# Gated cross-attention: x loaded a second time and transposed in 32x32 blocks on VectorE, scores computed transposed on two column halves of TensorE, tokens in pairs of tiles

## The chip, the cores and the metric

The kernel runs on one core of a Trainium2 chip. The metric is the device time of one execution in microseconds; lower is better. The time of the kernel before is the median of three runs, and one more execution was taken with the hardware profiler. All arithmetic is in 32-bit floats, in both kernels.

## What is computed

There are 8 batches of 1024 tokens with 1024 features (`x`), and for each batch 64 rows of memory with 512 features (`ctx_1024`).

```python
memory_proj = einsum('bme,de->bmd', memory, W_mem)                 # [8, 64, 1024]
scores = einsum('bnd,bmd->bnm', x, memory_proj) / sqrt(1024)       # [8, 1024, 64]
attn = softmax(scores, axis=-1)
memory_context = einsum('bnm,bmd->bnd', attn, memory_proj)         # [8, 1024, 1024]
gate_input = concatenate([x, memory_context], axis=-1)
gate = sigmoid(einsum('bnf,df->bnd', gate_input, W_gate) + b_gate) # W_gate [1024, 2048]
fused = x + gate * memory_context
out = fused * rsqrt(mean(fused**2, axis=-1) + 1e-6) * norm_w
```

## The kernel before

With mp = memory @ W_mem.T and W_gate = [W1 | W2], the second half of the gate's product is attn @ (mp @ W2.T). So a first stage computes, once for all batches, `mpT` (mp transposed, features on partitions: lines 108 to 122) and `mg` (for each batch 64 rows of mp over 64 rows of mp @ W2.T + bias: lines 124 to 153). This stage is the same work in both kernels; the steps that matter in it are the transposition of the memory into `memT` (`pt_mem`, L103 and L106), the product `pm` (L112) and the products `pg` of L142, whose results VectorE adds to the bias (L151).

Then come the tokens: 64 tiles of 128 tokens, four tiles to a group of 512, 16 groups. For each group `g`:

- `xg` holds its 512 rows of x, tokens on partitions, loaded in one transfer of 2 MB (`load_x`, four buffers).
- `scores(g, t)`: TensorE needs x with features on partitions. Eight transpositions of 128x128 (`pt`, L169) turn one tile; VectorE (L171) and ScalarE (L173) copy each half from PSUM into `xt` (two buffers, one for each of two groups). Then eight products of `xt` with `mpT` (L175) give the scores `sc` of the tile, 128 tokens on partitions by 64 columns.
- `softmax(g)`: over the group's four tiles at once, on VectorE and ScalarE; it writes `attn`.
- `transpose_attn(g)`: four transpositions on TensorE (`pa`, L206), and a copy on VectorE to `attnT` (L208).
- `fuse(g, t)`: 16 products of `xt` with W1 (`pg`, L223: eight for each of two halves of 512 columns), and then four products with 64 rows: two give the context `pc` (L235, rows 0 to 63 of the array), two add the gate's second half to `pg` (L236, rows 64 to 127). Sigmoid on ScalarE (L241), two multiplications and an addition on VectorE (L242, L243), the sum of squares on ScalarE (L244).
- `norm(g)`: square root on ScalarE, then one scaling for each tile on VectorE (L253) and its store.

The loop over the groups does `scores` and `softmax` of group g+1 between the tiles of `fuse` of group g. The order on each engine is made by a scheduler from the program, and each engine then runs its own queue in that order; SyncE (SP) issues all DMAs in order. In the trace every f32 product is two instructions on TensorE, each with its own weight load (a row with x16 is eight products); a transposition is one.

Of the kernel before, what the change touches and what calls it, by code (L numbers as in the profile page):

```python
# [8 lines left out]
F32 = mybir.dt.float32  # L9
# [5 lines left out]
P = 128  # L15
# [4 lines left out]
def tile_gated_cross_attention_rmsnorm(  # L20
    ctx: ExitStack,
    tc: tile.TileContext,
    x: bass.AP,  # [B, N, D]
    mem: bass.AP,  # [B, M, E]
    w_mem_t: bass.AP,  # [E, D]   W_mem transposed
    w_gate_t: bass.AP,  # [2D, D]  W_gate transposed
    b_gate: bass.AP,  # [D]
    norm_w: bass.AP,  # [D]
    out: bass.AP,  # [B, N, D]
):  # L30
    """Tokens lie on partitions, in groups of GT = 512.
# [10 lines left out]
    GT = 512  # L42
    TPG = GT // P  # tiles of 128 tokens in a group
    GPB = N // GT  # groups in a batch
    NG = B * GPB
# [5 lines left out]
    SCALE = 1.0 / float(D) ** 0.5  # L51

    const = ctx.enter_context(tc.tile_pool(name="const", bufs=1))
    xpool = ctx.enter_context(tc.tile_pool(name="xpool", bufs=4))
# [3 lines left out]
    ps_tr = ctx.enter_context(tc.tile_pool(name="ps_tr", bufs=2, space=PSUM))  # L58
    ps_sc = ctx.enter_context(tc.tile_pool(name="ps_sc", bufs=1, space=PSUM))
# [4 lines left out]
    mem_sb = xtpool.tile([P, NPAIR, E], F32, tag="xt", name="mem_sb")  # L64
    nc.sync.dma_start(mem_sb, mem.rearrange("b m e -> (b m) e").rearrange("(q p) e -> p q e", p=P))
    wm_sb = xpool.tile([P, KE, D], F32, tag="xg", name="wm_sb")
    nc.sync.dma_start(wm_sb, w_mem_t.rearrange("(k p) d -> p k d", p=P))

    def load_x(g):
        b, n0 = g // GPB, (g % GPB) * GT  # L70
        xg = xpool.tile([P, TPG, D], F32, tag="xg", name=f"xg{g}")
        nc.sync.dma_start(xg, x[b, n0 : n0 + GT, :].rearrange("(t p) d -> p t d", p=P))
        return xg

    xgs = {0: load_x(0)}

    bias_sb = const.tile([P, D], F32, name="bias_sb")
    nc.sync.dma_start(bias_sb, b_gate.partition_broadcast(P))
    w2_sb = []
    for h in range(NH):  # L80
        t = xpool.tile([P, KD, H], F32, tag="xg", name=f"w2_{h}")
        nc.sync.dma_start(t, w_gate_t[D:, h * H : (h + 1) * H].rearrange("(k p) f -> p k f", p=P))
        w2_sb.append(t)
    w1_sb = const.tile([P, KD, D], F32, name="w1_sb")
    for k in range(0, KD, 2):
        nc.sync.dma_start(
            w1_sb[:, k : k + 2, :],
            w_gate_t[k * P : (k + 2) * P, :].rearrange("(k p) f -> p k f", p=P),
        )
# [9 lines left out]
    memT = xtpool.tile([P, KE, BM], F32, tag="xt", name="memT")  # L99
    for k in range(KE):  # L100
        pt = ps_tr.tile([P, BM], F32, tag="tr", name=f"pt_mem{k}")
        for q in range(NPAIR):
            nc.tensor.transpose(  # L103
                pt[:, q * P : (q + 1) * P], mem_sb[:, q, k * P : (k + 1) * P], ident
            )
        nc.vector.tensor_copy(memT[:, k, :], pt)  # L106

    mpT = const.tile([P, KD, BM], F32, name="mpT")
    for d in range(KD):
        pm = ps_gate.tile([P, BM], F32, tag="gate", name=f"pm{d}")  # L110
        for k in range(KE):
            nc.tensor.matmul(  # L112
                pm,
                wm_sb[:, k, d * P : (d + 1) * P],
                memT[:, k, :],
                start=(k == 0),
                stop=(k == KE - 1),
            )
        if d % 2 == 0:
            nc.scalar.copy(mpT[:, d, :], pm)  # L120
        else:
            nc.vector.tensor_copy(mpT[:, d, :], pm)

    mg = const.tile([P, B, D], F32, name="mg")
    for q in range(NPAIR):
        for h in range(NH):
            cols = slice(h * H, (h + 1) * H)
            pt = ps_tr.tile([P, H], F32, tag="tr", name=f"pt_mp{q}_{h}")
            for j in range(H // P):
                nc.tensor.transpose(  # L130
                    pt[:, j * P : (j + 1) * P],
                    mpT[:, h * (H // P) + j, q * P : (q + 1) * P],
                    ident,
                )
            for i in range(2):
                nc.scalar.copy(mg[0:M, 2 * q + i, cols], pt[i * M : (i + 1) * M, :])  # L136
# [19 lines left out]
    xts, scs, attns, attnTs = {}, {}, {}, {}  # L156

    def scores(g, t):
        """x transposed, and the scores [128 tokens, M] of one tile."""
        b = g // GPB  # L160
        if t == 0:
            xts[g] = xtpool.tile([P, KD, GT], F32, tag="xt", name=f"xt{g}")
            scs[g] = ps_sc.tile([P, TPG, M], F32, tag="sc", name=f"sc{g}")
        xg, xt, sc = xgs[g], xts[g], scs[g]
        toks = slice(t * P, (t + 1) * P)
        for c in range(0, KD, 4):
            pt = ps_tr.tile([P, 4, P], F32, tag="tr", name=f"pt{g}_{t}_{c}")
            for j in range(4):
                nc.tensor.transpose(pt[:, j, :], xg[:, t, (c + j) * P : (c + j + 1) * P], ident)  # L169
            if c == 0:  # L170
                nc.vector.tensor_copy(xt[:, c : c + 4, toks], pt)  # L171
            else:
                nc.scalar.copy(xt[:, c : c + 4, toks], pt)  # L173
        for k in range(KD):
            nc.tensor.matmul(  # L175
                sc[:, t, :],
                xt[:, k, toks],
                mpT[:, k, b * M : (b + 1) * M],
                start=(k == 0),
                stop=(k == KD - 1),  # L180
            )

    def softmax(g):
        """attn of a group, twice side by side so that its transpose fills both row groups."""
        sc = scs.pop(g)
        mx = small.tile([P, TPG], F32, tag="mx", name=f"mx{g}")
        nc.vector.tensor_reduce(mx, sc, AX.X, ALU.max)
        e = small.tile([P, TPG, M], F32, tag="e", name=f"e{g}")
        nc.vector.tensor_tensor(e, sc, mx.unsqueeze(2).to_broadcast([P, TPG, M]), ALU.subtract)
        nc.scalar.activation(e, e, AF.Exp, scale=SCALE)  # L190
        den = small.tile([P, TPG], F32, tag="den", name=f"den{g}")
        nc.vector.tensor_reduce(den, e, AX.X, ALU.add)
        rden = small.tile([P, TPG], F32, tag="rden", name=f"rden{g}")
        nc.vector.reciprocal(rden, den)
        attn = small.tile([P, TPG, 2, M], F32, tag="attn", name=f"attn{g}")
        for i in range(2):
            nc.vector.tensor_tensor(
                attn[:, :, i, :], e, rden.unsqueeze(2).to_broadcast([P, TPG, M]), ALU.mult
            )
        attns[g] = attn  # L200

    def transpose_attn(g):
        attn = attns.pop(g)
        pa = ps_sc.tile([P, TPG, P], F32, tag="sc", name=f"pa{g}")
        for t in range(TPG):
            nc.tensor.transpose(pa[:, t, :], attn[:, t, :, :].rearrange("p i m -> p (i m)"), ident)  # L206
        attnT = small.tile([P, TPG, P], F32, tag="attnT", name=f"attnT{g}")
        nc.vector.tensor_copy(attnT, pa)  # L208
        attnTs[g] = attnT

    sss = {}

    def fuse(g, t):
        """xg[:, t] becomes x + gate * context, and its sum of squares is taken."""
        b = g // GPB
        if t == 0:
            sss[g] = small.tile([P, TPG], F32, tag="ss", name=f"ss{g}")
        xg, xt, attnT, ss = xgs[g], xts[g], attnTs[g], sss[g]
        pgs = []
        for h in range(NH):  # L220
            pg = ps_gate.tile([P, H], F32, tag="gate", name=f"pg{g}_{t}_{h}")
# [10 lines left out]
        for h in range(NH):  # L232
            cols = slice(h * H, (h + 1) * H)
            pc = ps_ctx.tile([P, H], F32, tag="ctx", name=f"pc{g}_{t}_{h}")
# [3 lines left out]
        gate = work.tile([P, D], F32, tag="gate", name=f"gate{g}_{t}")  # L238
# [7 lines left out]
    def norm(g):  # L246
        b, n0 = g // GPB, (g % GPB) * GT
        xg, ss = xgs.pop(g), sss.pop(g)
        rstd = small.tile([P, TPG], F32, tag="rstd", name=f"rstd{g}")
        nc.scalar.activation(rstd, ss, AF.Sqrt, bias=eps_sb, scale=1.0 / D)  # L250
        nc.vector.reciprocal(rstd, rstd)
        for t in range(TPG):
# [4 lines left out]
        del xts[g], attnTs[g]  # L257

    for t in range(TPG):
        scores(0, t)  # L260
    softmax(0)
    transpose_attn(0)
    for g in range(1, min(3, NG)):
        xgs[g] = load_x(g)
    for g in range(NG):
        nxt = g + 1 < NG
        for t in range(TPG):
            if nxt:
                scores(g + 1, t)
                if t == TPG - 1:  # L270
                    softmax(g + 1)
            fuse(g, t)
        if nxt:
            transpose_attn(g + 1)
        norm(g)
        if g + 3 < NG:
            xgs[g + 3] = load_x(g + 3)
# [26 lines left out]
```

## Time and profile before

| | |
|---|---|
| median of three runs | 1310.34 us (1309.6 to 1310.35) |
| the profiled execution: span from the first to the last instruction | 1308.3 us |
| the same execution's own time around the span | not listed; the median of the runs is 2.0 us above the span |
| TensorE products busy (PE) | 1284.8 us, 98% of the span |
| TensorE weight loads busy (PEld) | 644.2 us, 49% |
| VectorE busy (DVE) | 343.4 us, 26% |
| ScalarE busy (ACT) | 288.2 us, 22% |
| DMA | 80.33 MB, 61 GB/s over the span |
| granted TensorE clock | 0.995 (mean) |

How to read the rows. A row of the timeline has the start, the duration (of several merged instructions: from the first start to the last end), engine, line, operation, tiles (out<-in), shape and count; the bracket at the end is the engine's idle time before it and what ended it. A row of the groups has the busy time, the mean duration of one instruction in ns, and the idle time before. A row of the chain has start, duration and what ran. Matmuls are pipelined: the duration of one (594 ns for 512 columns) is longer than the distance between two, so the cost of a run of matmuls is read from the start of the run to the start of what follows it.

### The profile page before, as it was taken

To read this page: it belongs to the slowest core of one execution; us is meant where nothing else is said; L and a number is where in the kernel's file an instruction comes from. 1 tells how busy PE (TensorE), PEld (TensorE's weight loads), DVE (VectorE), ACT (ScalarE), POOL (GpSimd) and SP (SyncE) were. 2 spreads that over 40 slices of the span, in tenths; PEclk is the share of its full clock that TensorE was granted. 3 is DMA by queue.
4 is the path that set the end of the run, shared out by engine and by line. 5 is a ranking of instruction groups with operands and counts; after the bars stand their busy time and mean duration, and the time that the engine had idled before them with its cause. 6 is when DMAs were issued, how large, how long until landed. Compare 5 with 4: busy or idle time off the path is not lost.

```text
span 1308.3 us, 10030 instructions
## 1 busy us (share of the span) xinstructions
PE 1284.8 (98%) x4400; PEld 644.2 (49%) x4400; DVE 343.4 (26%) x472; ACT 288.2 (22%) x435; POOL 0.7 (0%) x7
## 2 busy tenths in 40 slices
PE   7999999999999999999999999999999999999995
PEld 3446555455545544555455545554555445544442
DVE  1122132132314122232313213231312313231413
ACT  0301131122213122122213122221213112221311
POOL 0000000000000000000000000000000000000000
PEclk9999999999999999999999999999999999999998
DMA  9311003030301103030200203030110301010101
GB/s 366 147 65 65 1 1 129 1 129 1 128 1 65 65 1 129 1 129 1 106 23 22 107 1 129 1 129 0 67 62 1 129 1 65 1 65 1 44 21 64
DMA packets 22220, 80.33 MB, mean 61 GB/s; under 512 B 1441, under 2 KB 1441, under 8 KB 22177
## 3 DMA queue, kind: packets, MB, share of 16 engines
q1 hardware_dynamic: 22176, 79.70, 15.8%
q8 instruction: 34, 0.56, 0.2%
q14 instruction: 10, 0.07, 0.0%
HBM read 46.14 MB, written 33.55 MB: 61 GB/s over the span
## 4 chain that ended last, share of the span: by engine, by line
PE 97%; DMA 1%; DVE 1%; ACT 1%; DVEq 0%; issue 0%; SPq 0%; ACTq 0%
PE pg L223 67%; PE pc L235 9%; PE sc L175 9%; PE pt L169 5%; PE pg L142 4%; PE pm L112 2%; DMA wm_sb<-in_w_mem_t 1%; PE pa L206 1%; DVE xg L253 0%; ACT mg L136 0%; PE pt_mp L130 0%; PE pg L236 0%; ACT L250 0%; DVE xg L243 0%; DVEq L300 0%; ACT gate L244 0%
## 5 line engine op out<-in xcount | busy, mean ns | idle before, releaser
L223 PE MATMUL pg<-w_sb,xt 128*128 128x512 f32 x2048 | 903.4, 594 | 0.0
L223 PEld LDWEIGHTS pg<-w_sb,xt 128*128 128x128 f32 x2048 | 379.3, 190 | 431.3 <-issue 429.0
L242 DVE TENSOR_TENSOR gate<-gate,pc 128x512 f32<-128x512 f32 x128 | 86.3, 684 | 791.0 <-ACT gate L241 790.8
L241 ACT ACTIVATE gate<-pg 128x512 f32<-128x512 f32 x128 | 74.8, 597 | 607.6 <-PE pg L236 607.5
L175 PEld LDWEIGHTS sc<-mpT,xt 128*128 128x128 f32 x1024 | 123.0, 192 | 34.2 <-DVE xt L171 24.6
L236 PE MATMUL pg<-mg,attnT 64*128 64x512 f32 x256 | 126.8, 615 | 0.0
L235 PE MATMUL pc<-mg,attnT 64*128 64x512 f32 x256 | 126.8, 615 | 0.0
L175 PE MATMUL sc<-mpT,xt 128*128 128x64 f32 x1024 | 123.0, 273 | 0.0
L244 ACT ACTIVATE gate<-xg 128x1024 f32<-128x1024 f32 x64 | 67.6, 1057 | 109.3 <-DVE xg L243 109.3
L235 PEld LDWEIGHTS pc<-mg,attnT 64*128 64x128 f32 x256 | 42.8, 186 | 78.7 <-issue 78.7
L243 DVE TENSOR_TENSOR xg<-xg,gate 128x1024 f32<-128x1024 f32 x64 | 78.1, 1220 | 1.2
L241 ACT ACT_TABLE_LOAD x31 | 39.8, 1283 | 174.5 <-PE pg L236 174.2
L253 DVE SCALAR_TENSOR_TENSOR xg<-xg,rstd,nw_sb 128x1024 f32<-128x1024 f32 x64 | 77.9, 1279 | 0.6
L169 PEld LDWEIGHTS pt<-ident,xg 128*128 128x128 f32 x512 | 55.9, 142 | 35.5 <-PE pg L236 33.4
L169 PE MATMUL pt<-ident,xg 128*128 128x128 f32 x512 | 69.4, 278 | 0.7 <-ACT xt L173 0.7
L142 PE MATMUL pg<-w,mpT 128*128 128x512 f32 x128 | 55.9, 592 | 0.0
L173 ACT COPY xt<-pt 128x512 f32<-128x512 f32 x64 | 37.6, 587 | 79.8 <-PE pt L169 79.8
L171 DVE COPY xt<-pt 128x512 f32<-128x512 f32 x64 | 44.0, 688 | 9.6 <-PE pt L169 6.7
L236 PEld LDWEIGHTS pg<-mg,attnT 64*128 64x128 f32 x256 | 42.8, 186 | 0.0
L142 PEld LDWEIGHTS pg<-w,mpT 128*128 128x128 f32 x128 | 23.9, 190 | 27.7 <-issue 27.7
L112 PE MATMUL pm<-memT,wm_sb 128*128 128x512 f32 x64 | 29.9, 630 | 1.2 <-DMA wm_sb<-in_w_mem_t 1.2
L151 DVE TENSOR_TENSOR mg<-pg,bias_sb 64x512 f32<-64x512 f32 x16 | 11.0, 690 | 48.9 <-PE pg L142 48.8
(31 smaller groups left out, 177.2 us busy)
## 6 DMA issues: line engine op xcount, KB each, us to landing
xg<-in_x SPq DMA_DIRECT2D x16, 2048.0 KB, 7.8
out<-xg SPq DMA_DIRECT2D x64, 512.0 KB, 2.8
w<-in_w_gate_t SPq DMA_DIRECT2D x2, 2048.0 KB, 22.2
w_sb<-in_w_gate_t SPq DMA_DIRECT2D x4, 1024.0 KB, 16.4
wm_sb<-in_w_mem_t SPq DMA_DIRECT2D x1, 2048.0 KB, 10.2
mem_sb<-in_mem SPq DMA_DIRECT2D x1, 1024.0 KB, 5.6
bias_sb<-in_b_gate SPq DMA_DIRECT2D x1, 512.0 KB, 15.5
nw_sb<-in_norm_w SPq DMA_DIRECT2D x1, 512.0 KB, 16.0
```

Source lines behind the costliest of these rows:

```text
L112: nc.tensor.matmul(pm, wm_sb[:, k, d * P : (d + 1) * P], memT[:, k, :], start=(k == 0), stop=(k == KE - 1),)
L142: nc.tensor.matmul(pg, mpT[:, k, q * P : (q + 1) * P], w2_sb[h][:, k, :], start=(k == 0), stop=(k == KD - 1),)
L169: nc.tensor.transpose(pt[:, j, :], xg[:, t, (c + j) * P : (c + j + 1) * P], ident)
L175: nc.tensor.matmul(sc[:, t, :], xt[:, k, toks], mpT[:, k, b * M : (b + 1) * M], start=(k == 0), stop=(k == KD - 1),)
L223: nc.tensor.matmul(pg, xt[:, k, t * P : (t + 1) * P], w1_sb[:, k, h * H : (h + 1) * H], start=(k == 0), stop=False,)
L235: nc.tensor.matmul(pc, attnT[0:M, t, :], mg[0:M, b, cols], start=True, stop=True)
L236: nc.tensor.matmul(pgs[h], attnT[M:P, t, :], mg[M:P, b, cols], start=False, stop=True)
L241: nc.scalar.activation(gate[:, cols], pgs[h], AF.Sigmoid)
L242: nc.vector.tensor_tensor(gate[:, cols], gate[:, cols], pcs[h], ALU.mult)
L243: nc.vector.tensor_tensor(xg[:, t, :], xg[:, t, :], gate, ALU.add)
L244: nc.scalar.activation(gate, xg[:, t, :], AF.Square, accum_out=ss[:, t : t + 1])
L253: nc.vector.scalar_tensor_tensor(xg[:, t, :], xg[:, t, :], rstd[:, t : t + 1], nw_sb, ALU.mult, ALU.mult)
```

## The change

Five things are changed together.

1. **x comes twice.** Beside `xg` (now 256 rows, a pair of tiles, 1 MB, four buffers) there is `xq` (two buffers): the same 256 rows, laid out so that partition 32i + c holds features 256i to 256i+255 of the tokens whose number is c modulo 32. It is loaded by four DMAs of 32 partitions each, in pieces of 1 KB.
2. **The transposition of x moves to VectorE.** For each pair, eight instructions of 128x256 transpose all 32x32 blocks of `xq` into `xt` (L203). The feature order in `xt` is a permuted one, so W1 and W2 are loaded with their rows in that order (eight DMAs of 32 partitions for each instead of four and two), and the columns of W_mem are permuted by four copies on VectorE (`wmp`, L142). The transpositions L169 on TensorE and the copies L171 and L173 are gone.
3. **The scores are computed transposed.** `mpT` is the stationary side (64 columns) and `xt` the moving one (128 tokens), so that the result is 64x128; the two tiles of a pair go to partitions 0 to 63 and 64 to 127 of one PSUM tile `psT`, on columns 0 to 63 and 64 to 127 of the array (L214). ScalarE copies it to `sT` (L222), and one transposition on TensorE turns it into `sc` (L228), tokens on partitions again.
4. **Pairs instead of groups.** Softmax, `transpose_attn`, `norm` and the stores are done for each of 32 pairs. The copy to `attnT` goes from VectorE to ScalarE (L251).
5. **The order.** `transpose_x` and `scores` of pair q+1 stand ahead of `fuse(q, 0)`, `softmax(q+1)` between the two tiles, `transpose_attn(q+1)` behind the second.

```diff
+    PT = 2 * P
+    PPB = N // PT
+    NQ = B * PPB
-    xpool = ctx.enter_context(tc.tile_pool(name="xpool", bufs=4))
+    big = ctx.enter_context(tc.tile_pool(name="big", bufs=2))
+    xqpool = ctx.enter_context(tc.tile_pool(name="xqpool", bufs=2))
+    xgpool = ctx.enter_context(tc.tile_pool(name="xgpool", bufs=4))
     xtpool = ctx.enter_context(tc.tile_pool(name="xtpool", bufs=2))
-    ps_tr = ctx.enter_context(tc.tile_pool(name="ps_tr", bufs=2, space=PSUM))
-    ps_sc = ctx.enter_context(tc.tile_pool(name="ps_sc", bufs=1, space=PSUM))
+    ps_sc = ctx.enter_context(tc.tile_pool(name="ps_sc", bufs=3, space=PSUM))
...
+    def load_xq(q):
+        b, n0 = q // PPB, (q % PPB) * PT
+        xq = xqpool.tile([P, S, Q4], F32, tag="xq", name=f"xq{q}")
+        src = x[b, n0 : n0 + PT, :].rearrange("(s c) (i e) -> i c s e", c=32, i=4)
+        for i in range(4):
+            nc.sync.dma_start(xq[32 * i : 32 * (i + 1), :, :], src[i])
+        return xq
...
+    wmp = []
+    for k in range(2):
+        t = xqpool.tile([P, 2, KD, P], F32, tag="xq", name=f"wmp{k}")
+        for c in range(2):
+            nc.vector.tensor_copy(
+                t[:, c, :, :].rearrange("p j (i r) -> p j i r", r=32),
+                wm[k][:, c, :].rearrange("p (i j r) -> p j i r", i=4, r=32),
+            )
+        wmp.append(t)
...
-        for c in range(0, KD, 4):
-            pt = ps_tr.tile([P, 4, P], F32, tag="tr", name=f"pt{g}_{t}_{c}")
-            for j in range(4):
-                nc.tensor.transpose(pt[:, j, :], xg[:, t, (c + j) * P : (c + j + 1) * P], ident)
-            if c == 0:
-                nc.vector.tensor_copy(xt[:, c : c + 4, toks], pt)
-            else:
-                nc.scalar.copy(xt[:, c : c + 4, toks], pt)
-        for k in range(KD):
-            nc.tensor.matmul(sc[:, t, :], xt[:, k, toks], mpT[:, k, b * M : (b + 1) * M], ...)
+    def transpose_x(q):
+        xq = xqs.pop(q)
+        xt = xtpool.tile([P, KD, PT], F32, tag="xt", name=f"xt{q}")
+        for s in range(S):
+            nc.vector.transpose(
+                xt[:, :, 32 * s : 32 * (s + 1)], xq[:, s, :].rearrange("p (j r) -> p j r", r=32)
+            )
+        xts[q] = xt
+
+    def scores(q):
+        b, xt = q // PPB, xts[q]
+        ps = ps_sc.tile([P, P], F32, tag="sc", name=f"psT{q}")
         for k in range(KD):
+            for t in range(2):
+                nc.tensor.matmul(
+                    ps[t * M : (t + 1) * M, :],
+                    mpT[:, k, b * M : (b + 1) * M],
+                    xt[:, k, t * P : (t + 1) * P],
+                    start=(k == 0),
+                    stop=(k == KD - 1),
+                )
+        sT = small.tile([P, P], F32, tag="sT", name=f"sT{q}")
+        nc.scalar.copy(sT, ps)
+        sTs[q] = sT
+
+    def softmax(q):
+        sc = ps_sc.tile([P, 2, M], F32, tag="sc", name=f"sc{q}")
+        nc.tensor.transpose(sc.rearrange("p t m -> p (t m)"), sTs.pop(q), ident)
...
-        nc.vector.tensor_copy(attnT, pa)
+        nc.scalar.copy(attnT, pa)
...
+    for q in range(NQ):
+        nxt = q + 1 < NQ
+        if q + 2 < NQ:
+            xqs[q + 2] = load_xq(q + 2)
+            xgs[q + 2] = load_xg(q + 2)
+        if nxt:
+            transpose_x(q + 1)
+            scores(q + 1)
+        fuse(q, 0)
+        if nxt:
+            softmax(q + 1)
+        fuse(q, 1)
+        if nxt:
+            transpose_attn(q + 1)
+        norm(q)
```

How the order moves, at three places (a row has the line, the operation, the tile it writes and those it reads, the shape and how many stand in a row; a number at the end of a name tells one buffer from another).

TensorE in the kernel before, from the last tile of one group to the first of the next; the next group's x is transposed and scored between the gate's products:

```order
L223 MATMUL pg_3_1_629<-w_sb,xt_327 128x512 x8
L235 MATMUL pc_3_0_638<-mg,attnT_426 128x512
L236 MATMUL pg_3_0_620<-mg,attnT_426 128x512
L235 MATMUL pc_3_1_641<-mg,attnT_426 128x512
L236 MATMUL pg_3_1_629<-mg,attnT_426 128x512
L206 MATMUL pa_651<-ident,attn_617 128x128 x4
L169 MATMUL pt_0_0_673<-ident,xg_430 128x128 x4
L169 MATMUL pt_0_4_679<-ident,xg_430 128x128 x4
L223 MATMUL pg_0_0_694<-w_sb,xt_432 128x512 x4
L175 MATMUL sc_672<-mpT,xt_671 128x64 x8
L223 MATMUL pg_0_0_694<-w_sb,xt_432 128x512 x4
```

TensorE in the changed kernel at the end of a pair; `psT_671` are the scores of the pair after the one whose gate products follow (`xt_538`), and its `xt_662` lies in the buffer that the first row reads as `xt_414`:

```order
L266 MATMUL pg_1_1_621<-w_sb,xt_414 128x512 x8
L278 MATMUL pc_1_0_630<-mg,attnT_522 128x512
L279 MATMUL pg_1_0_612<-mg,attnT_522 128x512
L278 MATMUL pc_1_1_633<-mg,attnT_522 128x512
L279 MATMUL pg_1_1_621<-mg,attnT_522 128x512
L249 MATMUL pa_643<-ident,attn_609 128x128 x2
L214 MATMUL psT_671<-xt_662,mpT 64x128 x16
L266 MATMUL pg_0_0_691<-w_sb,xt_538 128x512 x8
```

The score products now stand in one piece at the pair's end, between `pa` and the next gate products, with nothing else for TensorE to do ahead of them.

VectorE in the changed kernel at the same place of a later pair (with what each row waits for: `PE_49` is TensorE, `DMAHW` a transfer). The rows in front are the softmax of the pair before, those behind the elementwise part of the tile whose gate products have just ended:

```order
L240 TENSOR_TENSOR attn_981<-e_974,rden_979 128x2x64
L203 STREAM_TRANSPOSE xt_1034<-xq_903 128x8x32 [waits DMAHW4_49,DMAHW1_49,DMAHW7_49,DMAHW0_49,PE_49]
L203 STREAM_TRANSPOSE xt_1034<-xq_903 128x8x32 x7
L285 TENSOR_TENSOR gate_1_1008<-gate_1_1008,pc_1_0_1002 128x512 [waits Activation_49]
L285 TENSOR_TENSOR gate_1_1008<-gate_1_1008,pc_1_1_1005 128x512 [waits Activation_49]
L286 TENSOR_TENSOR xg_660<-xg_660,gate_1_1008 128x1024 [waits DVE_49]
```

In the kernel before, one PSUM copy of a tile (L171) stood at this place, behind the elementwise rows; now eight transpositions stand ahead of them, and their wait on TensorE is for the last gate product that reads the buffer they write.

VectorE in the changed kernel ahead of the first pair; the rows L190 are the last additions of the first stage (L151 before):

```order
L190 TENSOR_TENSOR mg<-pg_1_3_335,bias_sb 64x512 [waits PE_49]
L190 TENSOR_TENSOR mg<-pg_1_3_335,bias_sb 64x512
L203 STREAM_TRANSPOSE xt_356<-xq_346 128x8x32 [waits DMAHW6_49,DMAHW7_49,DMAHW5_49,DMAHW0_49]
L203 STREAM_TRANSPOSE xt_356<-xq_346 128x8x32 x7
L230 TENSOR_REDUCE mx_386<-sc_384 128x2 [waits PE_49]
```

The first pair's transposition stands behind the last addition, which waits for TensorE's last product of the first stage; in the kernel before, TensorE itself transposed the first tiles there.

More of the change, by code (lines that the diff above doesn't have):

```diff
@@ L196, in softmax, with transpose_attn @@
         for i in range(2):
             nc.vector.tensor_tensor(
-                attn[:, :, i, :], e, rden.unsqueeze(2).to_broadcast([P, TPG, M]), ALU.mult
+                attn[:, :, i, :], e, rden.unsqueeze(2).to_broadcast([P, 2, M]), ALU.mult
             )
[L200 to L205, printed above, removed]
+        attns[q] = attn
+    def transpose_attn(q):
+        attn = attns.pop(q)
+        pa = ps_sc.tile([P, 2, P], F32, tag="sc", name=f"pa{q}")
+        for t in range(2):
@@ L244, in fuse, with norm @@
         nc.scalar.activation(gate, xg[:, t, :], AF.Square, accum_out=ss[:, t : t + 1])
[L246 to L249, printed above, removed]
+    def norm(q):
+        b, n0 = q // PPB, (q % PPB) * PT
+        xg, ss = xgs.pop(q), sss.pop(q)
+        rstd = small.tile([P, 2], F32, tag="rstd", name=f"rstd{q}")
         nc.scalar.activation(rstd, ss, AF.Sqrt, bias=eps_sb, scale=1.0 / D)
         nc.vector.reciprocal(rstd, rstd)
-        for t in range(TPG):
+        for t in range(2):
             nc.vector.scalar_tensor_tensor(
```

151 lines of the change are left out of this document (66 added, 85 removed).

## The prediction

> **What bounds the kernel now.** I read the page's head and its chain first, to see which engine sets the time.
>
> ```profile
> span 1308.3 us, 10030 instructions
> PE 1284.8 (98%) x4400; PEld 644.2 (49%) x4400; DVE 343.4 (26%) x472; ACT 288.2 (22%) x435; POOL 0.7 (0%) x7
> PE 97%; DMA 1%; DVE 1%; ACT 1%; DVEq 0%; issue 0%; SPq 0%; ACTq 0%
> ```
>
> TensorE is on the chain for 97% of the span; what leaves its queue shortens the time, unless a wait takes its place. Busy time misleads for pipelined products, so I price them by distances between starts. Next the chain in order of time over one group (start, duration, what ran):
>
> ```profile
> 191.92 1.93 PE sc L175 x16
> ...
> 206.13 1.02 PE pt L169 x8
> ...
> 208.87 1.73 PE sc L175 x16
> 210.60 12.07 PE pg L223 x28
> ...
> 261.52 0.59 PE pa L206 x4
> ...
> 266.42 1.93 PE sc L175 x16
> ```
>
> The row at 191.92 comes back at 266.42: a group takes 74.50 us, without a gap. Sixteen score instructions take 208.87 to 210.60, or 0.108 each; 28 gate instructions 12.07, or 0.43 each. Last the timeline of TensorE in the last group, where no next group is transposed or scored:
>
> ```profile
> 1229.94 0.66 PE L206 MATMUL pa<-ident,attn 128*128 128x128 f32 x4
> 1230.43 1.02 PE L223 MATMUL pg<-w_sb,xt 128*128 128x512 f32 x2
> ...
> 1246.18 14.00 PE L223 MATMUL pg<-w_sb,xt 128*128 128x512 f32 x32
> 1260.11 0.69 PE L235 MATMUL pc<-mg,attnT 64*128 64x512 f32 x1
> 1260.11 0.69 PE L236 MATMUL pg<-mg,attnT 64*128 64x512 f32 x1
> ...
> 1262.03 1.55 PE L223 MATMUL pg<-w_sb,xt 128*128 128x512 f32 x3
> ```
>
> A tile with its gate and context alone takes 1246.18 to 1262.03, or 15.85 us; both kernels have 64 of these. `pc` and `pg` with 64 rows start together at 1260.11, so two halves of the array run side by side here. Four `pa` transpositions take 0.49 (1229.94 to 1230.43): 0.43 and some 0.06 of changeover.
>
> **The sum, part by part.**
>
> *Removed on TensorE.* A group of 74.50 less four tiles of 15.85 leaves 11.10 for its transpositions, scores and `pa`: 177.6 us for 16 groups. All of it is on the chain.
>
> *Added on TensorE, per pair.* `pa` of two: 0.27. `sc` of one: 0.17. `psT`: 16 products are 32 instructions. Each streams 128 columns where a gate instruction streams 512, so a quarter of 0.43: 0.108. If the column halves run side by side as the row halves do, that is 16 times 0.108 = 1.72; one behind the other it is 3.44. I take 1.72 by the nearest row, the pair at 1260.11, and both as ends. Beyond 3.44 lies an upper end: no overlap at all, each at the duration of a short product alone, 273 ns:
>
> ```profile
> L175 PE MATMUL sc<-mpT,xt 128*128 128x64 f32 x1024 | 123.0, 273 | 0.0
> ```
>
> That is 8.7 us a pair, 225 us more in all. For entering and leaving the halves I add 0.25: a tile has 32 times 0.43 and four times 0.43, or 15.48, and the other 0.37 of the 15.85 is its changeover into row halves and out; here the way in falls into the wait below. The Trainium skill, TensorEngine Tiling (Array Packing), section Key Properties, says that changing the tiling mode drains the engine: the trace agrees by that 0.37, and paying it in full here would add 4 us. The Trainium skill, TensorE: Matmul & The Clock Gate, section "Measured speedup vs the span model", has three 32-column tiles 2.38 times as fast, not three; two halves at the same share of ideal would give 1.6 times, and the sum would be 14 us higher. No row here shows column halves. Together 2.41 a pair, 77.1 for 32 pairs.
>
> *The new wait.* The transpositions of a pair write the `xt` buffer that the gate products just ended have read, and `psT`, next but for the context products and `pa`, needs all eight of them from its second product on. Ahead of it TensorE has only 1.92 (1260.11 to 1262.03) and 0.27. The price on VectorE is not in the trace. Nearest are ops of the same 128x256, and one of twice the length:
>
> ```profile
> L197 DVE TENSOR_TENSOR attn<-e,rden 128x256 f32<-128x256 f32 x32 | 12.2, 422 | 0.6
> L208 DVE COPY attnT<-pa 128x512 f32<-128x512 f32 x16 | 11.0, 684 | 0.8 <-PE pa L206 0.8
> ```
> ```profile
> 622.33 0.76 DVE L197 TENSOR_TENSOR attn<-e,rden 128x256 f32<-128x256 f32 x2
> ```
>
> From 256 to 512 elements an op grows by 262 ns, so about 1.02 ns an element; 1024 would take about 1.2 us. Two independent ops of 256 end in 0.76, 0.34 behind each other. Eight are 7 x 0.34 + 0.42 = 2.8 at that pace, 8 x 0.42 = 3.4 with no overlap; I take 3.1. The bounds lie further out: two elements a step would halve it to 1.6, and four steps an element (a 1024-wide op each) would make it 9.8. The Trainium skill, VectorE: DVE Perf Modes, section The three transpose paths, gives 311 ns for 128x128 in bf16; an estimate of 0.44 for twice the elements would put the sum 13 us higher.
>
> The ends of the wait:
>
> ```profile
> 99.68 1.02 PE L142 MATMUL pg<-w,mpT 128*128 128x512 f32 x2
> 100.74 0.69 DVE L151 TENSOR_TENSOR mg<-pg,bias_sb 64x512 f32<-64x512 f32 x1 [5.47 <-PE pg L142]
> ...
> 616.18 0.69 DVE L171 COPY xt<-pt 128x512 f32<-128x512 f32 x1
> 616.31 0.30 PEld L223 LDWEIGHTS pg<-w_sb,xt 128*128 128x128 f32 x2
> 616.42 1.02 PE L223 MATMUL pg<-w_sb,xt 128*128 128x512 f32 x2
> 616.93 0.19 PEld L175 LDWEIGHTS sc<-mpT,xt 128*128 128x128 f32 x1 [0.32 <-DVE xt L171]
> ```
>
> VectorE starts 0.04 after a product's end, a weight load 0.06 after VectorE's, a product 0.11 after its load. The last gate product of a tile ends at 1260.18 (1246.18 + 14.00); VectorE has nothing else, since the softmax ahead of it ended long before. 1260.18 + 0.04 + 3.1 + 0.17 = 1263.49, against 1260.11 + 1.92 + 0.27 = 1262.30. So TensorE waits 1.2 us, in 30 pairs (the first two have free buffers): 36 us. VectorE's elementwise ops stand behind the transpositions, 3 us later; the PSUM that they free is wanted a tile, 15 us, later.
>
> *Start.* One transfer of W_mem becomes two, and four 1024-wide copies on VectorE must run ahead of most of `pm`.
>
> ```profile
> 6.50 3.84 PE L103 MATMUL pt_mem<-ident,mem_sb 128*128 128x128 f32 x16 [6.50 <-DMA mem_sb<-in_mem]
> 7.62 0.69 DVE L106 COPY memT<-pt_mem 128x512 f32<-128x512 f32 x1 [7.62 <-PE pt_mem L103]
> 11.51 29.91 PE L112 MATMUL pm<-memT,wm_sb 128*128 128x512 f32 x64 [1.17 <-DMA wm_sb<-in_w_mem_t]
> ```
>
> The 2 MB land at 11.5, 5 us after the memory's 1 MB, so the first half at about 9. Then VectorE does four copies of 1.2 and four of 0.69, 7.6 us, to 16.5. By then TensorE has done three products, 2.6 us. It is 16.5 - 2.6 - 11.5 = 2.4 later. At two elements a step it would be about nothing.
>
> *First pair.* At 100.70 TensorE went from L142 straight to `pt`. Now it waits for VectorE's two last additions (0.04 + 2 x 0.69), eight transpositions and 0.17: 4.7 us. The wait of 0.9 that the first group's softmax cost (16 x 74.50 from 100.70 is 1292.7, the products end at 1293.6) goes, since four gate products stand beside that chain now.
>
> *End.* The last `norm` scales two tiles, not four:
>
> ```profile
> 1293.20 0.59 PE L236 MATMUL pg<-mg,attnT 64*128 64x512 f32 x1
> ...
> 1299.45 4.87 DVE L253 SCALAR_TENSOR_TENSOR xg<-xg,rstd,nw_sb 128x1024 f32<-128x1024 f32 x4
> ```
>
> Two of 1.2 are 2.4 less.
>
> *At nothing.* ScalarE's table loads go from 63 to 127, and at
>
> ```profile
> L241 ACT ACT_TABLE_LOAD x31 | 39.8, 1283 | 174.5 <-PE pg L236 174.2
> ```
>
> 64 more are 82 us on an engine that is 22% busy. At a pair's end the sigmoids may come 1.3 later; the gate product that wants their PSUM stands behind `pa`, `psT` and eight gate products (6.9 us). Without that cover it would be 1.3 x 32 = 41 us. The `sT` copy is wanted 15 us later, `attnT` 14. x comes twice, 1 MB more a pair in pieces of 1 KB:
>
> ```profile
> xg<-in_x SPq DMA_DIRECT2D x16, 2048.0 KB, 7.8
> w<-in_w_gate_t SPq DMA_DIRECT2D x2, 2048.0 KB, 22.2
> ```
> ```profile
> 11.50:50.00 38.50, 38.05 (x107) 18.13 (x108) 2.77 (x4) 10.12 (x18) 0.00 (x0) 1.00 0.90 345
> ```
>
> An `xq` buffer is free once its pair is transposed and wanted two pairs later, 70 us. Each pair's last quarter and its `xg` stand in SP's queue behind two stores that wait for `norm`, some 12 us after the pair's end; even 22 us to land leaves 35. W2 is wanted from about 44 us and W1 from 103; at the 345 GB/s of the last row (the stretch 11.5 to 50 us) their 8 MB take 24 us, and they stand ahead of `xq` in the queue. If an `xq` came 10 us late each time it would cost 300 us; I see nothing that makes it so.
>
> *The sum:* 1308.3 - 177.6 + 77.1 + 36 + 2.4 + 4.7 - 0.9 - 2.4 = 1247.6 of span. The median of the runs stands 2.0 above the profiled span: 1250.
>
> **Rivals.** (a) *The column halves run one behind the other.* All eight k-steps read the same 128 partitions for both halves, unlike the row halves at 1260.11, which read different ones. Then 1.72 x 32 = 55 more: 1305. (b) *The transpositions are dear, and it ends slower.* A 32x32 block must be full before it can be written, and 4-byte data may need two passes. At the 684 of a 512-wide op, eight take 5.5, the wait grows by 2.4 in 30 pairs and the first: 1324. It decides from 0.63 us for each: 60 us more over 31 places is 1.94, or 5.04 for eight. Against it: the 128x256 ops all take 422. (c) *The wait is hidden.* With eight transpositions in 1.9 us or less TensorE never waits: 1213. It needs more than one element a step, which no VectorE row here shows. (d) *Both (a) and (b)*: about 1380, or halves that don't overlap at all, to 1475.
>
> **How the numbers follow.** My forecast, side by side and about one element a step, gets 0.60; its own range is 1232 (transpositions at 2.8, W_mem copies twice as fast) to 1276 (the halves 1.6 times as fast, transpositions at 3.6). (a) 0.16, around 1305; (b) 0.13; (c) 0.05; (d) 0.06. The range 1228 to 1318 takes the forecast, nearly all of (a) and the near part of (b). What 0.2% can tell is 2.6 us: faster means below 1307.7. Faster: 0.60 + 0.05 + two thirds of (a) = 0.76; the same 0.05 from (a) and (b); slower 0.19.
>
> **What would show it.** In the changed kernel's groups, L203 at 0.35 to 0.45 us; `psT` in the timeline, pairs of starts 0.108 apart for 1.7 us, and a weight load of L214 that waits for VectorE about 1.2 us at every pair's end, with gate products right behind. The period of a pair should be 35.3 us against 37.25. It would be wrong if L214 takes 3.4 us or more, if L203 takes 0.63 us or more, or if L203 waits for a transfer instead of TensorE.

## The result, and the profile after

The changed kernel takes 1225.81 us (median of 4 runs, 1225.63 to 1226.71), the kernel before 1309.97 in the same comparison: 0.9361 times, with a 95% interval of 0.9348 to 0.9374. The forecast was 1250, in the right direction, 24 us too high, and the result lies 2 us below the low end of its range. The profiled execution has a span of 1223.9 us, 84.4 below the 1308.3 of before.

The head of the page, DMA queue 1, and the chain by engine:

```profile
span 1223.9 us, 9771 instructions
PE 1195.8 (98%) x3920; PEld 541.1 (44%) x3920; DVE 385.8 (32%) x764; ACT 361.1 (30%) x531; POOL 0.7 (0%) x7
q1 hardware_dynamic: 57424, 113.26, 31.3%
PE 91%; DVE 7%; ACT 1%; DMA 1%; issue 0%; DVEq 0%; SPq 0%; ACTq 0%
```

TensorE is busy for 98% of the span, as before, but only 91% of the chain is its own: VectorE, which had 1%, has 7%. The chain in order of time over one pair (start, duration, what ran), and its last product:

```profile
592.37 1.96 PE psT L214 x30
594.33 13.93 PE pg L266 x32
...
610.18 0.26 PE sc L228
610.44 13.75 PE pg L266 x32
624.19 0.02 issue
624.21 2.74 DVE xt L203 x8
626.96 0.04 issue
627.00 1.96 PE psT L214 x30
...
1211.98 0.03 PE pg L279
```

From 592.37 to 627.00 a pair takes 34.63 us; two tiles took 37.25 before, and the forecast was 35.3. At each pair's end the chain leaves TensorE for the eight transpositions on VectorE: 2.74 us, which stand where context products and `pa` run beside them. How much of that is a real wait the timeline of the same place tells (the bracket is the engine's idle time):

```profile
624.21 2.73 DVE L203 STREAM_TRANSPOSE xt<-xq 128x256 f32<-128x256 f32 x8 [9.99 <-PE pg L266]
...
626.02 0.44 PE L249 MATMUL pa<-ident,attn 128*128 128x128 f32 x2
626.39 0.43 PE L214 MATMUL psT<-xt,mpT 128*64 128x128 f32 x2
627.00 1.72 PEld L214 LDWEIGHTS psT<-xt,mpT 128*64 128x64 f32 x30 [0.42 <-DVE xt L203]
627.00 1.96 PE L214 MATMUL psT<-xt,mpT 128*64 128x128 f32 x30 [0.18 <-DVE xt L203]
628.89 2.41 PE L266 MATMUL pg<-w_sb,xt 128*128 128x512 f32 x5
```

The first two `psT` instructions need only the first tile's transpositions and start at 626.39; the other 30 start at 627.00, 0.06 after VectorE's end. They take 1.89 to the first gate product at 628.89; with three buffers, below, all 32 take 1.90. So the pair loses 627.00 - 626.39 = 0.61 us. The bracket of PE shows 0.18 of it, because the end of the two instructions ahead is modelled: a wait is better read from the start of the work that was held back. The groups give the prices of single operations:

```profile
L203 DVE STREAM_TRANSPOSE xt<-xq 128x256 f32<-128x256 f32 x256 | 87.4, 408 | 299.8 <-PE pg L266 299.8
L142 DVE COPY wmp<-wm_sb 128x1024 f32<-128x1024 f32 x4 | 2.7, 687 | 8.8 <-DMA wm_sb<-in_w_mem_t 8.8
```

One transposition of 128x256 lasts 408 ns in the mean, but eight end in 2.74 us: (2.74 - 0.41) / 7 = 0.333 from one to the next. L203 waits for TensorE and no transfer. The start and the first pair, in the timeline (first product of `pm`; last additions of the first stage and what follows):

```profile
11.04 3.18 PE L152 MATMUL pm<-memT,wmp 128*128 128x512 f32 x4
...
99.62 1.39 DVE L190 TENSOR_TENSOR mg<-pg,bias_sb 64x512 f32<-64x512 f32 x2 [5.47 <-PE pg L181]
101.03 2.73 DVE L203 STREAM_TRANSPOSE xt<-xq 128x256 f32<-128x256 f32 x8
102.60 0.66 PE L214 MATMUL psT<-xt,mpT 128*64 128x128 f32 x2 [3.02 <-DVE xt L203]
```

`pm` starts at 11.04, where it started at 11.51 before, and at 102.60 TensorE has been idle for 3.02 us. Four stretches around it, and one of a pair in the middle (busy time of PE, PEld, DVE, ACT, POOL with their counts, then the granted clock, DMA share and GB/s):

```profile
97.00:99.60 2.60, 2.58 (x7) 0.80 (x5) 0.00 (x0) 0.00 (x0) 0.00 (x0) 1.00 0.00 0
99.60:102.60 3.00, 0.00 (x0) 0.03 (x1) 2.95 (x7) 0.00 (x0) 0.00 (x0) 0.97 0.00 0
102.60:105.30 2.70, 2.70 (x6) 0.87 (x8) 1.16 (x4) 0.00 (x0) 0.00 (x0) 0.50 0.10 23
105.30:108.00 2.70, 2.70 (x32) 2.29 (x33) 0.00 (x0) 0.27 (x1) 0.00 (x0) 0.91 1.08 236
...
605.00:640.00 35.00, 34.82 (x117) 15.73 (x116) 11.45 (x23) 10.96 (x16) 0.00 (x0) 1.00 0.31 93
```

After 3.0 us without work the clock is 0.50 for 2.7 us and 0.91 in the mean of the next 2.7, which costs another 1.6 (an estimate: 2.7 x 0.50 and 2.7 x 0.09). The 0.61 us wait at a pair's end, within the last row, leaves it at 1.00.

### The profile page after: what moved, and what is told of

Its sections match the earlier page's. It is cut to its first block, busy times and chain, and to the rows that moved or that the text cites. A ratio compares the mean times of both kernels' runs of the same rounds, so it can differ in the third digit from the quotient of the medians.

```text
span 1223.9 us, 9771 instructions
## 1 busy us (share of the span) xinstructions
PE 1195.8 (98%) x3920; PEld 541.1 (44%) x3920; DVE 385.8 (32%) x764; ACT 361.1 (30%) x531; POOL 0.7 (0%) x7
## 4 chain that ended last, share of the span: by engine, by line
PE 91%; DVE 7%; ACT 1%; DMA 1%; issue 0%; DVEq 0%; SPq 0%; ACTq 0%
PE pg L266 73%; DVE xt L203 7%; PE pc L278 5%; PE psT L214 5%; PE pg L181 4%; PE pm L152 2%; PE sc L228 1%; DMA wm_sb<-in_w_mem_t 1%; ACT mg L172 0%; PE pt_mp L169 0%; DVE xg L296 0%; ACT L293 0%; DVE xg L286 0%; DVEq L345 0%; ACT gate L287 0%
## 5 line engine op out<-in xcount | busy, mean ns | idle before, releaser
L266 PEld LDWEIGHTS pg<-w_sb,xt 128*128 128x128 f32 x2048 | 385.5, 191 | 463.8 <-issue 463.8
L203 DVE STREAM_TRANSPOSE xt<-xq 128x256 f32<-128x256 f32 x256 | 87.4, 408 | 299.8 <-PE pg L266 299.8
L230 DVE TENSOR_REDUCE mx<-sc 128x2 f32<-128x128 f32 x32 | 9.4, 293 | 324.0 <-PE sc L228 324.0
L285 DVE TENSOR_TENSOR gate<-gate,pc 128x512 f32<-128x512 f32 x128 | 81.1, 671 | 33.0 <-ACT gate L284 33.0
L214 PE MATMUL psT<-xt,mpT 128*64 128x128 f32 x1024 | 77.1, 278 | 8.2 <-DVE xt L203 8.2
L214 PEld LDWEIGHTS psT<-xt,mpT 128*64 128x64 f32 x1024 | 61.5, 137 | 24.4 <-DVE xt L203 12.5
L222 ACT COPY sT<-psT 128x128 f32<-128x128 f32 x32 | 8.5, 266 | 125.5 <-PE psT L214 125.5
L294 DVE RECIPROCAL rstd<-rstd 128x2 f32<-128x2 f32 x32 | 5.3, 166 | 90.4 <-ACT rstd L293 90.4
```

What stands on the lines that cost most here:

```text
L203: nc.vector.transpose(xt[:, :, 32 * s : 32 * (s + 1)], xq[:, s, :].rearrange("p (j r) -> p j r", r=32))
L214: nc.tensor.matmul(ps[t * M : (t + 1) * M, :], mpT[:, k, b * M : (b + 1) * M], xt[:, k, t * P : (t + 1) * P], start=(k == 0), stop=(k == K ...
L266: nc.tensor.matmul(pg, xt[:, k, t * P : (t + 1) * P], w1_sb[:, k, h * H : (h + 1) * H], start=(k == 0), stop=False,)
L285: nc.vector.tensor_tensor(gate[:, cols], gate[:, cols], pcs[h], ALU.mult)
```

## The experiments

The runs were made in three comparisons, each beside runs of the kernel before on the same chip (its medians there: 1308.13 us beside three buffers, each transposition twice, the loop over the tiles outside and VectorE's transposition alone; 1308.17 beside the column halves, the pairs and x loaded once; 1309.7 beside half the transpositions and the first pair earlier). In brackets behind a time stands its share of the kernel before in the same comparison, with the 95% interval. Each expectation names its theories; where it says no more, A is that the gain is three separate things, transpositions and copies that leave TensorE, scores side by side on column halves, and less a wait that is just VectorE's duration beyond TensorE's own work.

**Three buffers for `xt`.** The transpositions then needn't wait for the last gate product.

```diff
-    xtpool = ctx.enter_context(tc.tile_pool(name="xtpool", bufs=2))
+    xtpool = ctx.enter_context(tc.tile_pool(name="xtpool", bufs=3))
```

> A third xt buffer, so that the eight transpositions of a pair can run a tile earlier and TensorE finds them done. Theory A (the wait of TensorE for the transpositions at every pair's end is on the path, and what the trace of the changed kernel shows of it, about 0.4 us in 30 pairs, is its whole price): 12 us less, 1214 us. Rival B (that gap is TensorE's own changeover from pa into the column halves): no change, 1226 us. Had my prediction's 1.2 us a pair been right, it would be 36 us less, 1190 us.

Measured: 1208.09 us (0.9233 of before, 0.9217 to 0.9248), faster than both kernels. The chain of the pair's end:

```profile
616.09 0.37 PE pa L249 x2
616.46 1.90 PE psT L214 x32
...
650.49 1.56 PE psT L214 x25
```

VectorE is gone from it, and the period is 650.49 - 616.46 = 34.03, 0.60 below the changed kernel's. That is the 0.61 read above: the wait is worth 18 us in 30 places, not the 36 of the forecast. The other 1.6 of the 19.6 us between the spans lie ahead of the first pair, where the first stage ended earlier (its last product at 97.8 instead of 99.6). There `pm` starts at 10.57 and lasts 27.66 us, in the changed kernel at 11.04 and 28.93, for the same 64 products. The third buffer is not the cause: the run with the loop over the tiles outside has two buffers and the same early stage (10.60, 27.65), the last run below has three and the late one (11.14, 28.98). What sets the pace there is open.

**Half the transpositions.** Is the wait their duration, or the way from engine to engine and back? The second tile's four are left out; its score and gate products read the first tile's columns (the last edit shown stands at both).

```diff
-        for s in range(S):
+        for s in range(S // 2):
             nc.vector.transpose(
...
-                    xt[:, k, t * P : (t + 1) * P],
+                    xt[:, k, 0:P],
```

> The changed kernel with only the first four of a pair's eight VectorE transpositions; the second tile's transpositions are left out, and its scores and gate products read the first tile's columns of xt, so the work of TensorE is the same in number, size and order. Theory A: the wait of 0.60 us at a pair's end is the duration of the eight transpositions (2.74 us) less what TensorE still has to do beside them; four take 3 x 0.333 + 0.41 = 1.41 us, which ends before pa does, so the wait goes in 30 places (18 us) and the first pair starts 1.3 us earlier: 1207 us, the period of a pair 34.03 us. Theory B: the wait is the way from TensorE to VectorE and back (semaphores, a weight load that can't run ahead), whatever the transpositions take: 1222 to 1226 us, period 34.6.

Measured: 1207.43 us (0.9224, 0.921 to 0.9237). The timeline shows the transpositions and two starts of `psT`:

```profile
614.87 1.42 DVE L203 STREAM_TRANSPOSE xt<-xq 128x256 f32<-128x256 f32 x4 [9.99 <-PE pg L266]
...
617.04 1.97 PE L214 MATMUL psT<-xt,mpT 128*64 128x128 f32 x32
651.07 1.97 PE L214 MATMUL psT<-xt,mpT 128*64 128x128 f32 x32
```

Four end 1.42 after their start, well ahead of 617.04, and the period is 34.03 again. With two `xt` buffers and the same way from TensorE to VectorE and back the wait is gone; it was the duration. The first pair did not start earlier, against the expectation: its first `psT` needs only the first four transpositions in the changed kernel too.

**Each transposition twice.**

```diff
-            nc.vector.transpose(
+            for _ in range(2):
+                nc.vector.transpose(
```

> Each of the eight transpositions of a pair is done twice into the same place (16 instructions, same result). Theory A (every further microsecond of transposition at the pair's end is a microsecond of TensorE's waiting): 2.7 us more in 30 pairs and the first, 83 us, 1309 us. Rival B (hidden beside other work): 1226 us. Theory C (a wait of some 3 us also halves the granted clock for what follows, as the first pair's wait of 3.0 us does in the changed kernel's trace, 0.50 over the next 2.7 us): another 1.3 us or so a pair, 1350 us.

Measured: 1251.48 us (0.9563, 0.9549 to 0.9577), which no theory had. The chain says why:

```profile
638.10 4.03 DVE xt L204 x12
642.13 1.17 DVE gate L286 x2
...
645.47 0.46 DVE xt L204
...
645.98 1.96 PE psT L215 x30
647.94 9.64 PE pg L267 x22
```

The scheduler made another order: only 22 of a tile's 32 gate instructions stand behind `psT` here, ten run ahead of it while VectorE works, and VectorE's own elementwise rows come between the transpositions. So this run doesn't isolate the duration (the two above do). It shows by accident that gate products can cover transpositions: 16 transpositions and three elementwise operations fill VectorE from 638.10 to 645.93, and the pair is longer by 0.80 us only (610.55 to 645.98 is 35.43). Nor does it test theory C: TensorE's longest pause in a pair is 0.63 us here, and the granted clock is 1.00 from 605 to 640.

**The loop over the tiles outside the loop over k.** The two halves then alternate only once.

```diff
-        for k in range(KD):
-            for t in range(2):
+        for t in range(2):
+            for k in range(KD):
```

> The same 16 score products, but all eight of the first tile ahead of all eight of the second, so that neighbours in the queue lie on the same column half. Theory A (the two halves run side by side, and that is worth half of 32 times 0.108 us): 1.7 us more a pair, 55 us, 1281 us. Rival B (the shorter score stage comes from the 64-column weight loads, not from two halves at once): no change, 1226 us.

Measured: 1250.98 us (0.9555, 0.9541 to 0.9569). Chain:

```profile
601.75 3.26 PE psT L214 x32
...
637.14 3.26 PE psT L214 x32
```

The same 32 instructions take 3.26 us instead of 1.90: neighbours on different column halves run side by side, neighbours on the same half one behind the other. The price is 1.36 a pair, and 1246.7 - 1204.3 (the spans of this run and of three buffers) = 42.4 is 31 times that. I had expected 1281, since the order does a second thing: the first 16 instructions now need only the first tile's transpositions, and the wait of 0.61 goes. 3.26 - 1.90 - 0.61 = 0.75, and 30 times that is 22.5, near the 22.8 by which the span grew (the first pair's dearer scores and a first stage that ended 1.7 us earlier go opposite ways).

**VectorE's transposition alone.** The scores as before (`xt` stationary, `mpT` moving, tokens on partitions at once):

```diff
-        for k in range(KD):
-            for t in range(2):
+        for t in range(2):
+            for k in range(KD):
...
-                    ps[t * M : (t + 1) * M, :],
-                    mpT[:, k, b * M : (b + 1) * M],
-                    xt[:, k, t * P : (t + 1) * P],
+                    sc[:, t, :],
+                    xt[:, k, t * P : (t + 1) * P],
+                    mpT[:, k, b * M : (b + 1) * M],
```

> The transposition on VectorE is kept, the scores are computed as before (xt stationary, 64 columns of mpT moving, tokens on partitions), without psT, its copy and its transposition. Theory A (each part's worth is the distance its instructions take on TensorE): scores 3.46 us a pair in place of 1.89 + 0.17, so 1.4 more, 45 us, 1271 us. Rival B (the gain is all from moving the transposition): 1226 us or a little less, for the transposition of sT goes.

Measured: 1254.51 us (0.9588, 0.9574 to 0.9603). Chain:

```profile
607.44 3.52 PE sc L214 x32
...
642.89 3.52 PE sc L214 x32
```

`sc` at 3.52 us for two tiles is before's price, 32 times 0.108 and some changeover, though only 64 columns stream. As above there is no wait in this order, which is why it came below the expected 1271. The half clock behind the first wait lasts longer here: 0.50 in all stretches from 102.4 to 111 us and 0.67 from 111 to 113, some 3.4 us dearer than in the changed kernel (an estimate: 8.6 x 0.50 and 2 x 0.33, less 1.6).

**The column halves alone, and pairs alone.** Both start from the kernel before with groups of two tiles; the second changes nothing more, the first computes the scores as the changed kernel does, from x transposed on TensorE.

```diff
-    GT = 512
+    GT = 256
...
-            nc.tensor.matmul(
-                sc[:, t, :],
-                xt[:, k, toks],
-                mpT[:, k, b * M : (b + 1) * M],
+            for u in range(2):
+                nc.tensor.matmul(
+                    ps[u * M : (u + 1) * M, :],
+                    mpT[:, k, b * M : (b + 1) * M],
+                    xt[:, k, u * P : (u + 1) * P],
```

> The kernel before in pairs of tiles with x transposed on TensorE, and only the scores changed: transposed, the two tiles on the column halves, with psT, its copy and one transposition back. Theory A: against the kernel before, scores of 3.46 us a pair become 1.89 + 0.17 and one more changeover of about 0.2, so 1.2 less, 38 us, 1272 us. Rival B (the halves pay only together with the transposition on VectorE): 1310 us.

> The kernel before with groups of two tiles in place of four and nothing else changed. Theory A (the grouping is worth only the changeovers of pa and the shorter end: plus 0.8 us and minus 2.4 us): 1309 us. Rival B (smaller groups bring more stalls from softmax and ScalarE's table loads on TensorE's path, 1.3 us a pair): 1350 us.

Measured: 1276.74 us (0.9753, 0.9738 to 0.9767) with halves, 1302.02 (0.9949, 0.9934 to 0.9964) with pairs only. Chain of the first, then of the second:

```profile
629.66 1.02 PE pt L168 x8
630.69 0.36 PE psT L178 x2
...
632.97 1.89 PE psT L178 x30
...
667.02 0.36 PE psT L178 x2
```
```profile
606.34 1.03 PE pt L169 x8
...
609.08 1.73 PE sc L175 x16
...
643.49 1.02 PE pt L169 x8
```

Periods of 36.33 and 37.15. With pairs as the common ground the parts stand in a square: neither 1302.0, halves alone 25.3 less, VectorE alone 47.5 less, both (the changed kernel) 76.2 less. The sum of the parts is 72.8, but it comes so near by chance: the changed kernel pays the wait of 18 us, which the run with VectorE alone doesn't have. With three buffers both are worth 93.9, and a pair gains 1.42 by the halves (35.45 to 34.03), against 0.82 beside TensorE's transpositions (37.15 to 36.33). So the halves are worth more once the transposition is on VectorE, 0.60 in 32 pairs or 19 of the 21 us between the sums; the longer half clock of the run with VectorE alone is in them too. That `psT` stands in two pieces with gate instructions between (0.36 and 1.89) in the run with halves alone may be the reason; no run shows it. Pairs themselves bring 6, where I had expected about nothing.

**x loaded once for the scores.** Beyond the first two pairs nothing is loaded into `xq`.

```diff
+    xqs01 = [xqs[0], xqs[1]]
...
-            xqs[q + 2] = load_xq(q + 2)
+            xqs[q + 2] = xqs01[q % 2]
```

> The changed kernel without the second load of x after the first two pairs: every later pair transposes the rows of the first two, so its scores and gates are those of other tokens. All instructions on the engines stay. Theory A (the 32 MB more are hidden): 1226 us. Rival B (the second load slows the other transfers or the engines' access to memory): faster by what it costs, and I know no size for it; over 3 us would count.

Measured: 1226.94 us (0.9374, 0.9358 to 0.939). From the page:

```profile
span 1223.9 us, 9588 instructions
q1 hardware_dynamic: 24784, 81.80, 20.0%
```

31.5 MB less, and the same span to the tenth: the second load is hidden entirely.

**The first pair earlier.** Three buffers, and the first pair's transpositions ahead of the last additions of the first stage:

```diff
+    for q in range(2):
+        xqs[q] = load_xq(q)
...
     for h in range(NH):
...
+        if h == 1:
+            transpose_x(0)
```

> The kernel with three xt buffers, and with the first pair's transpositions ahead of VectorE's last additions of the first stage (x is loaded ahead of W1 for that). Theory A: the 3.0 us in which TensorE waits for the first pair, and the 2.7 us at half clock behind them (1.4 us lost), go: 4.4 us less than the 1208 us of three buffers alone; but the scheduler now puts the first softmax between score and gate products with nothing beside it, some 2.5 us, so 1206 us, with no stretch at clock 0.50. Theory B: the half clock follows from the change of work and not from the wait: no gain, 1208 us or, with the softmax bare, 1211 us.

Measured: 1212.22 us (0.9262, 0.9246 to 0.9277), 4 more than three buffers alone had in another comparison; the two intervals just overlap. The timeline of TensorE:

```profile
99.65 1.97 PE L216 MATMUL psT<-xt,mpT 128*64 128x128 f32 x32
101.98 0.33 PE L230 MATMUL sc<-ident,sT 128*128 128x128 f32 x1 [0.37 <-ACT sT L224]
104.41 0.44 PE L251 MATMUL pa<-ident,attn 128*128 128x128 f32 x2 [2.10 <-DVE attn L242]
...
111.11 0.41 PE L251 MATMUL pa<-ident,attn 128*128 128x128 f32 x2 [2.19 <-DVE attn L242]
```

The wait of 3.02 and the half clock are gone (all 2 us stretches from 92 to 112 have a clock of 1.00), so theory B, that the half clock follows from the change of work, falls. But the order that came of it leaves two softmax chains bare, 2.10 and 2.19 us, where I had counted one. Not a gain: three `xt` buffers remain the best version, 1208.09 us.

## Why the prediction came out 24 us high

*Right.* TensorE stays the bound; the column halves run side by side; a new wait for VectorE appears at every pair's end, after `pa`, with the cause given; the second load is hidden, and so is ScalarE's work (1% of the chain).

*Right by luck.* The first pair was to pay 4.7 us and pays about 4.6. But the forecast had eight transpositions ahead of its first score product where the trace has four, so that TensorE idles 3.0 us, and the half clock behind that pause, 1.6 us, stood nowhere in the sum.

*The step that failed is "The new wait": "I take 3.1", between 2.8 and 3.4.* TensorE was to wait 1.2 us at 30 pairs' ends, 36 us in all; it waits 0.61, which is 18. The largest piece of the difference is the eight transpositions, 2.73 instead of 3.1. The row quoted there, two independent operations ending in 0.76, gave 2.8 by itself; taking the middle gave half weight to an end, no overlap at all, that this row already contradicted. Next, 0.17 was charged from VectorE's end to the product, a weight load and then a product; here load and product start together at 627.00, 0.06 after VectorE. And TensorE's cover was 0.09 longer. There `pa` takes 0.37 (626.02 to 626.39) instead of 0.27; in the run with the scores as before it takes 0.28 (607.00 to 607.28), so the 0.09 lie in the way into the column halves. 0.37 + 0.11 + 0.09, and 0.01 at VectorE's start, is the 0.58 from 1.19 to 0.61. Times 30 that is 18 of the 24 us: a small misjudgment at a place that repeats.

The ends of the forecast's own range don't come out of its terms either. Transpositions at 2.8 and the faster copies take 9.3 and 2.4 off 1250, which is 1238 and not 1232; halves at 1.6 times and transpositions at 3.6 add 14 and 15.5, which is 1280 and not 1276. The result lies below both low ends.

*The rest.* "Start" forecast +2.4 and gave -1.1: from 11.04 instead of 11.51 for `pm` to 99.59 instead of 100.70 for the end of the stage's last product. The `wmp` copies took 687 ns for 1024 elements, not 1.2 us, which is the end that the forecast named, at "about nothing", and did not take. The other 1.1 us were in no argument: `pm` took 28.93 us for the work that took 29.91 before and 27.66 with three buffers. The Trainium skill, VectorE: DVE Perf Modes, section "Mode 2×_2P — use both read ports for one tensor", says that a copy with its one source and its destination in SBUF moves two elements a step; the 687 ns agree, since an operation of 512 from PSUM takes as long (684). The sum without the wait was 34.11 a pair and is 34.03 in the run with three buffers: 2.5 us over 31 pairs. The end, 1211.98 to 1223.9, is 2.6 shorter than before (1293.79 to 1308.3) instead of 2.4. Together 18 + 3.5 + 2.5 + 0.2 = 24.2, against 1247.6 - 1223.9 = 23.7; the first pair's 0.1 goes the same way, so about half a microsecond is unassigned.

*The rivals.* (a), halves one behind the other, falls: 1.90 us, not the 3.26 of the run in blocks. Nor would it have been 1305: with the changed kernel's order and its wait of 0.61, 1.36 more in 32 pairs give an estimate of 1269, and the order that makes them serial also takes the wait away, 1251. (b), dear transpositions, falls: 0.333 us apart, far from the 0.63 where it decides. The estimate of 0.44 from the bf16 figure of the Trainium skill, VectorE: DVE Perf Modes, section The three transpose paths, is near the 0.41 that one lasts and above the spacing. (c), the wait hidden, did not come: its condition was 1.9 us for all eight, and they take 2.74. But it named only one way to that end; a third buffer hides the wait at the same 2.74, and the time is then 1208 against its 1213.

The 1.97 taken for `psT` and its changeover is 1.90, and 1.99 with the 0.09 in `pa`. The Trainium skill, TensorE: Matmul & The Clock Gate, section "Measured speedup vs the span model", led to an estimate of 1.6 times for two halves; measured is 3.26 / 1.90 = 1.72. The way into the halves and out costs 0.27 by these rows, the 0.18 that 1.90 has above 1.72 and the 0.09. The Trainium skill, TensorEngine Tiling (Array Packing), section Key Properties, states that a change of the tiling mode drains the engine; a drain here is within that 0.27.

## What to carry to other kernels

Where work moves off the bounding engine, the gain is what its rows cost there; the loss is one subtraction at the place where the two engines meet, the helper's duration less what the bound has left to do, and it is worth pricing to a tenth of a microsecond when it repeats 30 times. Take the spacing of operations back to back, not the mean of one. Before accepting such a wait, ask which buffer makes the helper start late: here one more `xt` buffer was worth 18 us.

## What the runs showed of the hardware that was not expected

- Two 64-column halves of the array run side by side for products that read the same 128 partitions, if neighbours in the queue alternate: 32 instructions of 128 columns in 1.90 us, against 3.26 in blocks of 16 for each half.
- `psT` streams twice the columns of `sc` at about the same price per instruction: 3.52 us for 32 with 64 columns, 0.110 each, and 3.26 for 32 with 128 columns, 0.102 each. From 128 to 64 columns the price did not fall. Whether the weight load sets it was not tried.
- A pause of 3.0 us was enough for half clock over the next 2.7 us, pauses of 2.1 and 2.2 were not (clock 1.00). The Trainium skill, TensorE: Matmul & The Clock Gate, section Part 1: The HAM clock gate, gives an idle window of about 3.4 us that runs freely; the 3.0 us agree only if such a window need not be idle from end to end, and no run here settles that.
- The same 3.02 us pause with three buffers had a clock of 0.72 in the following 2.7 us and 0.66 in the 2.8 after them, so when the half clock begins is not fixed by the pause alone. It lasted 3.4 us in both (0.50 from 102.42 to 105.83 in the changed kernel, from 102.0 to 105.4 with three buffers), but over 8.6 us behind the same pause in the run with VectorE's transposition alone (0.50 from 102.4 to 111).

```profile
100.80:103.50 2.70, 2.65 (x14) 1.55 (x16) 1.21 (x4) 0.00 (x0) 0.00 (x0) 0.72 0.08 16
103.50:106.30 2.80, 2.80 (x26) 2.39 (x23) 0.00 (x0) 0.27 (x1) 0.00 (x0) 0.66 1.02 227
```
